# Attention and clustering block, first image: where the score units of the first steps stand between the value products

## The chip, the cores and the metric

The kernel runs on one core of one Trainium2 chip. A core has a matrix engine (TensorE, PE in the profile; its weight loads are the row PEld), a vector engine (VectorE, DVE), a scalar engine for activations (ScalarE, ACT), GpSimd (POOL), and SyncE (SP), which here issues transfers. Each engine runs its own instructions in the order of the program and waits for the others by semaphores. The metric is the device time of one execution in microseconds (us), the median of three runs.

## The reference: what is computed

The input is x of shape (4, 256, 64, 64): four images, 256 channels, N = 4096 positions each. Two layers follow. The change lies in the first, which is self-attention over the positions of one image:

```python
xf = x.reshape(B, Cc, N)
q = jnp.einsum('oc,bcn->bno', wq, xf) + bq            # 32 channels
k = jnp.einsum('oc,bcn->bon', wk, xf) + bk[None, :, None]
attn = jax.nn.softmax(jnp.einsum('bnd,bdm->bnm', q, k), axis=-1)
v = jnp.einsum('oc,bcn->bon', wv, xf) + bv[None, :, None]
out = jnp.einsum('bcn,bmn->bcm', v, attn).reshape(B, Cc, H, W)
return gamma[0] * out + x
```

The second layer, per image, is a group norm, a clustering step (each position is given to one of four centres per head by cosine similarity, centres are averaged and handed back), a second group norm, an MLP 256 to 1024 to 256 with GELU, and two scaled ReLU stages with a 256 to 256 product between them. All is float32.

## The kernel before

The images are worked through one after the other. For each: projections to q, k and v; the attention loop (`weighting`); `cluster`; `mlp`. The projections and the first scores of images 1 to 3 are laid into the clustering and MLP of the image before. Image 0 has no image before it, so `alone` makes its projections and its first scores with nothing beside them.

The attention of an image is cut into 8 query blocks (`nb`) of 512 queries, and for each block into 8 groups (`g`) of 512 keys. A pair of block and group is one unit, `u = 8 * nb + g`, so there are 64 units. The code handles a unit three times, in different places:

- `score(u)` (L359 to L384) makes the 512 x 512 scores. Four 32-row products go side by side into two PSUM tiles of two banks each, `halves[0]` and `halves[1]`. The pool `ps_s` has room for just these two tiles, so the next unit can begin only when both are read. Each half is read twice: ScalarE copies it to an SBUF slot (L377 for the first half, L382 for the second), and VectorE takes the running maximum over keys (L381 from the second half, L384 from the first; for a group 0, L379 alone).
- `exps(u)` (L452 to L468), once the maximum of the block is known: VectorE subtracts it (L460, two halves), ScalarE takes the exponential in place (L463, two halves), GpSimd adds the result to a running total `acc` (L465, L468).
- `weigh(u, av, quarter)` (L470 to L479): the value products. A unit has four quarters of 128 keys. A quarter is two products in the code, which the profile shows as four instructions on TensorE.

`weighting` (L576) runs one step per unit. Step u first issues `exps(u + 1)` and then the four quarters of `weigh(u)`. Between the quarters stand calls `due(u, quarter)` (L569), which issue the score unit, if any, that the table `at` names for this place; after the last score of a block they also call `fold`, the first part of the block's final maximum. Usually it is unit u + 10 (`LEAD`), ahead of quarter 0 of step u. The order of instructions is written out by hand in this way: the scheduler is off (`tc.manual_schedule()`), and each engine gets its instructions in the order in which the Python code runs.

For images 1 to 3 (`b` not zero) the first steps are different: the MLP of the image before has already scored units 0 to 7, and units 8 to 15 are put at the quarter indices 2, 4, 7, 10, 13, 16, 18 and 21, counted from step 0 (`(14 * i + 10) // 5`, L565). For image 0, `alone` scores units 0 to 8. Then L567 puts unit 9 ahead of quarter 0 of step 0 and unit 10 ahead of quarter 2. Image 0 also has a special order in step 0 (L598 to L600): quarters 0 and 1 of the value products are issued ahead of `due(0, 0)`, and the general place (L606 to L609) is skipped. So units 9 and 10 follow each other directly in step 0, after quarter 1. From step 1 on unit u + 10 comes ahead of quarter 0 of step u.

Three other things stand near. After step 1, image 0 runs `early()`, which is `derived` (L194 to L224): some fifteen small VectorE operations on weights of 128 x 2 elements, two square roots on ScalarE that need another function table, two transposes and a small product on TensorE, and two copies of their results. From step 3 on, `biased` steps add the value bias to x on ScalarE (L632), and step 3 fetches the queries of block 2 (L638). And in step 5 `highest` (L433) begins to work out the maximum of block 1, which needs units 8 to 15.

Of the kernel before, what the change touches and what calls it, by code (L numbers as in the profile page):

```python
# [28 lines left out]
RG, GRP = 4, N // NB  # L29
# [16 lines left out]
def attention_then_cluster_block(  # L46
# [78 lines left out]
    def load_mix(b):  # L125
        own_w["mix"] = swap.tile([P, KC, 2, 2 * ED + 32], F32, tag="mix", name=f"mix_{b}")
        for f in range(2):
            nc.sync.dma_start(
                out=own_w["mix"][:, :, f, 16 : 16 + 2 * ED],
                in_=wfv.rearrange("(k p) m -> p k m", p=P),  # L130
            )
# [139 lines left out]
    def attention(b, xs):  # L271
# [76 lines left out]
        def score(u, hooks=None, later=None):  # L348

            nb, g = divmod(u, GRP)  # L350
            q_s, k_s = qs[nb], own["k"]
            pool, tag = (swap, "w1") if u % (SLOTS + 1) == SLOTS else (spool, "s")
            s = slots[u] = pool.tile([P, RG, NB], F32, tag=tag, name=f"s_{b}_{u}")
            halves = [
                ps_s.tile([P, 2, NB], F32, tag="s", name=f"sc_{b}_{u}_{h}") for h in range(2)
            ]
            for r in range(RG):
                rows = slice(r * D, (r + 1) * D)
                nc.tensor.matmul(  # L359
                    halves[r // 2][:, r % 2, :], k_s[rows, g, :], q_s[rows, :], start=True, stop=True  # L360
                )
            if g == 0:
                tops[nb] = work.tile([P, 2, NB], F32, tag="top", bufs=1, name=f"top_{b}_{nb}")
            top = tops[nb]
            if hooks is not None:

                nc.scalar.copy(s[:, 0:2, :], halves[0])
                hooks.append(lambda: nc.scalar.copy(s[:, 2:4, :], halves[1]))
                for h in range(1 if g == 0 else 0, 2):
                    for i in range(2):  # L370
                        later.append(
                            lambda h=h, i=i: nc.vector.tensor_tensor(
                                top[:, i], s[:, i] if g == 0 else top[:, i], s[:, 2 * h + i], ALU.max
                            )
                        )
                return
            nc.scalar.copy(s[:, 0:2, :], halves[0])  # L377
            if g == 0:
                nc.vector.tensor_tensor(top, halves[1], s[:, 0:2, :], ALU.max)  # L379
            else:  # L380
                nc.vector.tensor_tensor(top, halves[1], top, ALU.max)  # L381
            nc.scalar.copy(s[:, 2:4, :], halves[1])  # L382
            if g:
                nc.vector.tensor_tensor(top, halves[0], top, ALU.max)  # L384

        def fold(nb):

            top = tops[nb]
            nc.vector.tensor_tensor(top[:, 0], top[:, 0], top[:, 1], ALU.max)
# [80 lines left out]
        def weigh(u, av, quarter):  # L470
            g = u % GRP
            for c in range(KC):
                nc.tensor.matmul(  # L473
                    av[c],
                    own["v"][:, RG * g + quarter, c * P : (c + 1) * P],
                    slots[u][:, quarter, :],
                    start=(g == 0 and quarter == 0),
                    stop=(g == GRP - 1 and quarter == RG - 1),
                )  # L479

        def gather(nb):

            acc = accs.pop(nb)
            rdens[nb] = work.tile([P, NB], F32, tag="rden", bufs=1, name=f"rden_{b}_{nb}")
            nc.gpsimd.tensor_tensor(rdens[nb], acc[:, 0], acc[:, 1], ALU.add)
# [75 lines left out]
        at = {(u, 0): u + LEAD for u in range(units - LEAD)}  # L561
        if b:
            for i in range(6):
                del at[i, 0]
            at.update({divmod((14 * i + 10) // 5, RG): GRP + i for i in range(8)})  # L565
        else:
            at[0, 2], at[0, 0] = at[0, 0], GRP + 1  # L567

        def due(u, quarter):  # L569
            p = at.get((u, quarter))  # L570
            if p is not None:
                score(p)
                if p % GRP == GRP - 1:
                    fold(p // GRP)

        def weighting(ahead, fill, early):  # L576
            mb, av = None, None

            biased = {u: (i // KC, i % KC) for i, u in enumerate((3, 4, 5, 6, 20, 28, 36, 44))}
            for u in range(units):  # L580
                nb, g = divmod(u, GRP)
                more = nb + 1 < NBLK
                if g == 0:
                    av = [
                        ps_a.tile([P, NB], F32, tag=f"a{c}", name=f"av{c}_{b}_{nb}")
                        for c in range(KC)
                    ]
                if g + 1 < GRP:
                    exps(u + 1)
                else:  # L590
                    gather(nb)
                p = u + LEAD
                if u == units - 4:
                    load_mix(b)
                    load_mlp(b)
                elif u == units - 1:
                    turn_mlp()
                if u == 0 and not b:  # L598
                    weigh(u, av, 0)
                    weigh(u, av, 1)  # L600
                due(u, 0)
                if p - units > 1:
                    ahead()
                if g == GRP - 1 and more:
                    exps(u + 1)
                if u or b:  # L606
                    weigh(u, av, 0)
                    due(u, 1)
                    weigh(u, av, 1)  # L609
                if nb:  # L610
                    if g == 0:
                        total(nb - 1)
                    elif g == 3:
                        add(nb - 1)
                    elif g == 5:
                        seen(nb - 1)
                    elif g == 7:
                        pooled(nb - 1)
                due(u, 2)
                weigh(u, av, 2)  # L620
                if g == GRP - 2 and more:
                    known(nb + 1, mb)
                due(u, 3)
                if g == GRP - 3 and more:
                    mb = highest(nb + 1)
                weigh(u, av, 3)
                if u == 1:
                    early()
                if u in biased:

                    t, c = biased[u]
                    nc.scalar.activation(  # L632
                        xs[t][:, c], xs[t][:, c], AF.Identity, bias=gbv[:, c : c + 1]
                    )
                if u == 2 * GRP + 1:
                    q_four(1)
                if g == 3 and nb + 2 < NBLK:
                    q_block(nb + 2)  # L638
                if g == GRP - 1 and more:
                    clear(nb, av)  # L640

            nb = NBLK - 1
            table(AF.Sqrt)

            den = ps_m.tile([P, NB], F32, tag="m", name=f"den_{b}_{nb}")
            for j in range(4):
                nc.tensor.matmul(
                    den[j * D : (j + 1) * D, :P],
                    ones[:, :D],
                    rdens[nb][:, j * P : (j + 1) * P],  # L650
                    start=True,
                    stop=True,
                )
            fill(2)
            t_s = work.tile([P, KC, NB], F32, tag="t", bufs=1, name=f"t_{b}_{nb}")
            rec = t_s[:, 1, :P]
            nc.vector.reciprocal(rec, den[:, :P])

            inv = ps_m.tile([P, NB], F32, tag="m", name=f"inv_{b}_{nb}")
            for j in range(4):  # L660
                nc.tensor.matmul(
                    inv[:, j * P : (j + 1) * P],
                    ident[:, j * D : j * D + 1].to_broadcast([P, P]),
                    rec,
                    start=True,
                    stop=True,
                )
            rden = rdens[nb]
            nc.scalar.copy(rden, inv)
            fill(6)  # L670
            for c in range(KC):
                yb = block(xs, c, nb)
                nc.vector.tensor_tensor(t_s[:, c], av[c], rden, ALU.mult)
                nc.vector.scalar_tensor_tensor(
                    yb, t_s[:, c], pvc("gamma"), yb, ALU.mult, ALU.add
                )
            seen(nb)
            return stats, cells, lambda: pooled(nb)
# [768 lines left out]
```

## Time and profile before

| what | us |
|---|---|
| median of three runs | 3419.7 (3418.95 to 3419.9) |
| the profiled execution | 3419.29 |
| its span on the core | 3417.5 |
| stretch from 61.5 to 109.5 us, TensorE busy | 44.99 of 48.00 |
| stretch from 109.5 to 285 us, TensorE busy | 175.50 of 175.50 |
| one score unit's maximum over one half (L381), mean | 1.221 |
| one score unit's copy of one half (L377), mean | 1.004 |
| one subtraction of a half (L460), mean | 1.205 |
| one exponential of a half (L463), mean | 1.057 |
| one subtotal on GpSimd (L468), mean | 2.360 |

The page's table of slices shows the same thing at a coarse scale. The span is cut into 40 equal slices, and each digit is the busy share of an engine in tenths:

```profile
PE   8999999999999999999999999999999999999999
DVE  4667764655566766464556676646546766765543
ACT  5555543444555554344455555434446555544444
POOL 2655665210265666521125566652004675672200
PEclk9999999999999999999999999999999999999999
```

A slice is about 85 us. The first one holds the loads, `alone` and the first two steps of image 0's attention loop. A start time and a duration in the timeline are in us from the start of the span; several equal instructions in a row are put together as "x8". A duration of such a group runs to the modelled end of its last instruction, and may overlap the next row by some hundred ns.

### The profile page before, as it was taken

To read this page: it belongs to the slowest core of one execution; us is meant where nothing else is said; L and a number is where in the kernel's file an instruction comes from. 1 tells how busy PE (TensorE), PEld (TensorE's weight loads), DVE (VectorE), ACT (ScalarE), POOL (GpSimd) and SP (SyncE) were. 2 spreads that over 40 slices of the span, in tenths; PEclk is the share of its full clock that TensorE was granted. 3 is DMA by queue.
4 is the path that set the end of the run, shared out by engine and by line. 5 is a ranking of instruction groups with operands and counts; after the bars stand their busy time and mean duration, and the time that the engine had idled before them with its cause. 6 is when DMAs were issued, how large, how long until landed. Compare 5 with 4: busy or idle time off the path is not lost.

```text
span 3417.5 us, 31890 instructions
## 1 busy us (share of the span) xinstructions
PE 3363.0 (98%) x11536; PEld 1663.4 (49%) x11536; DVE 2069.2 (61%) x3219; ACT 1674.2 (49%) x2157; POOL 1490.3 (44%) x807
## 2 busy tenths in 40 slices
PE   8999999999999999999999999999999999999999
PEld 4434445665533444565544344466554343445565
DVE  4667764655566766464556676646546766765543
ACT  5555543444555554344455555434446555544444
POOL 2655665210265666521125566652004675672200
PEclk9999999999999999999999999999999999999999
DMA  2000002000000000100000000010000000010000
GB/s 71 13 13 10 16 7 85 7 19 13 19 13 13 13 13 22 70 7 19 19 16 13 10 13 13 22 70 7 19 19 13 13 13 13 13 36 1 13 19 25
DMA packets 41501, 70.01 MB, mean 20 GB/s; under 512 B 9632, under 2 KB 16896, under 8 KB 41344
## 3 DMA queue, kind: packets, MB, share of 16 engines
q1 hardware_dynamic: 36480, 61.16, 5.3%
q10 hardware_dynamic: 4608, 6.30, 0.8%
q8 instruction: 91, 1.49, 0.2%
q0 software_dynamic: 256, 0.52, 0.1%
q14 instruction: 66, 0.54, 0.1%
HBM read 42.68 MB, written 16.89 MB: 17 GB/s over the span
## 4 chain that ended last, share of the span: by engine, by line
PE 95%; DVE 3%; ACT 1%; issue 0%; DMA 0%; SPq 0%; ACTq 0%; DVEq 0%
PE av L473 53%; PE mo L1204 12%; PE sc L359 8%; PE hu L1197 4%; PE pw L1173 3%; PE hp L1197 3%; PE hq L1197 3%; PE vp L310 2%; PE fv L859 2%; PE op L980 1%; PE qp L329 0%; PE kp L287 0%; DVE vf L868 0%; DVE hs L1233 0%; PE agg L889 0%
## 5 line engine op out<-in xcount | busy, mean ns | idle before, releaser
L473 PE MATMUL av<-s,v 128*128 128x512 f32 x4096 | 1820.5, 598 | 0.6 <-ACT s L463 0.6
L468 POOL TENSOR_TENSOR acc<-acc,s 128x1024 f32<-128x1024 f32 x448 | 1057.3, 2360 | 543.2 <-ACT s L463 524.4
L473 PEld LDWEIGHTS av<-s,v 128*128 128x128 f32 x4096 | 759.8, 190 | 1045.4 <-issue 1035.4
L463 ACT ACTIVATE s<-s 128x1024 f32<-128x1024 f32 x512 | 540.1, 1057 | 592.7 <-DVE s L460 549.7
L460 DVE TENSOR_TENSOR s<-s,mb 128x1024 f32<-128x1024 f32 x512 | 595.5, 1205 | 17.8 <-ACT mb L444 15.9
L1204 PE MATMUL mo<-hs,w 128*128 128x512 f32 x992 | 508.3, 595 | 3.8 <-ACT hs L1226 1.6
L381 DVE TENSOR_TENSOR top<-sc,top 128x1024 f32<-128x1024 f32 x196 | 239.4, 1221 | 377.9 <-PE sc L359 377.8
L1226 ACT ACTIVATE hs<-hs,pv_s 128x256 f32<-128x256 f32 x496 | 251.4, 508 | 361.1 <-DVE hs L1233 350.1
L1233 DVE TENSOR_TENSOR hs<-hu,hs 128x256 f32<-128x256 f32 x372 | 157.7, 424 | 356.2 <-ACT hs L1236 205.5
L377 ACT COPY s<-sc 128x1024 f32<-128x1024 f32 x224 | 224.8, 1004 | 228.8 <-PE sc L359 228.8
L1159 POOL TENSOR_TENSOR xn<-xn 128x256 f32<-128x256 f32 x27 | 23.9, 884 | 682.4 <-DVE xn L1146 488.0
L359 PE MATMUL sc<-q,k 32*128 32x512 f32 x2048 | 294.4, 640 | 3.0 <-ACT s L382 3.0
L384 DVE TENSOR_TENSOR top<-sc,top 128x1024 f32<-128x1024 f32 x196 | 240.0, 1224 | 72.6 <-ACT s L377 59.4
L382 ACT COPY s<-sc 128x1024 f32<-128x1024 f32 x224 | 227.0, 1014 | 66.2 <-DVE top L379 36.1
L465 POOL TENSOR_TENSOR acc<-s 128x1024 f32<-128x1024 f32 x32 | 75.3, 2354 | 366.8 <-ACT s L463 366.7
L1233 DVE TENSOR_TENSOR hs<-hq,hs 128x256 f32<-128x256 f32 x372 | 146.3, 421 | 107.5 <-PE hq L1197 103.2
L1204 PEld LDWEIGHTS mo<-hs,w 128*128 128x128 f32 x992 | 186.9, 190 | 42.6 <-ACT hs L1236 7.8
L359 PEld LDWEIGHTS sc<-q,k 32*128 32x128 f32 x2048 | 81.8, 182 | 193.7 <-issue 141.5
L1197 PE MATMUL hp<-xn,w 128*128 128x256 f32 x496 | 150.6, 385 | 2.6 <-ACT v L318 2.6
L1197 PEld LDWEIGHTS hp<-xn,w 128*128 128x128 f32 x496 | 92.4, 190 | 73.0 <-issue 62.5
L310 PE MATMUL vp<-wv_s,x 128*128 128x256 f32 x512 | 123.4, 387 | 0.2 <-ACT v L318 0.2
L1173 PE MATMUL pw<-xn,wpw_s 128*128 128x512 f32 x248 | 112.0, 594 | 3.4 <-ACT xn L1267 2.2
(219 smaller groups left out, 2737.7 us busy)
## 6 DMA issues: line engine op xcount, KB each, us to landing
x<-in_x SPq DMA_DIRECT2D x32, 512.0 KB, 6.6
out<-xn SPq DMA_DIRECT2D x62, 256.0 KB, 2.1
w<-in_w SPq DMA_DIRECT2D x8, 1024.0 KB, 10.2
mr<-row_mx SPq DMA_DIRECT2D x28, 256.0 KB, 3.1
rden<-row_rd SPq DMA_DIRECT2D x28, 256.0 KB, 3.1
q<-q ACTq DMA_DIRECT2D x96, 64.0 KB, 2.0
mix<-in_wfv SPq DMA_DIRECT2D x8, 192.0 KB, 8.1
q<-q SPq DMA_DIRECT2D x24, 64.0 KB, 2.0
```

What stands on the lines that cost most here:

```text
L359: nc.tensor.matmul(halves[r // 2][:, r % 2, :], k_s[rows, g, :], q_s[rows, :], start=True, stop=True)
L381: nc.vector.tensor_tensor(top, halves[1], top, ALU.max)
L382: nc.scalar.copy(s[:, 2:4, :], halves[1])
L384: nc.vector.tensor_tensor(top, halves[0], top, ALU.max)
L460: nc.vector.tensor_tensor(sh, sh, mxs[nb].unsqueeze(1).to_broadcast([P, 2, NB]), ALU.subtract)
L463: nc.scalar.activation(sh, sh, AF.Exp)
L468: nc.gpsimd.tensor_tensor(acc, acc, s[:, 2 * h : 2 * h + 2], ALU.add)
L473: nc.tensor.matmul(av[c], own["v"][:, RG * g + quarter, c * P : (c + 1) * P], slots[u][:, quarter, :], start=(g == 0 and quarter == 0), st ...
L1197: nc.tensor.matmul(out, w[:, j * P : (j + 1) * P], x, start=True, stop=True)
L1204: yield nc.tensor.matmul(acc[c], w2_s[:, jj, c * P : (c + 1) * P], hs[:, i], start=(j == 0 and i == 0), stop=(j == HID // P // 2 - 1 and i ...
L1226: nc.scalar.activation(dst, src, act, bias=bias)
L1233: nc.vector.tensor_tensor(dst, ps, term, ALU.add)
```

## The change

It concerns image 0 only. The table of score places is set anew for its first steps: the entries for quarter 0 of steps 0 to 5 are taken out, and units 9 to 15 are put at the quarter indices 2, 5, 8, 11, 14, 17 and 20, that is ahead of (step, quarter) (0, 2), (1, 1), (2, 0), (2, 3), (3, 2), (4, 1) and (5, 0). The special order of step 0 is taken out as well, so that step 0 has the general order: due, quarter 0, due, quarter 1, due, quarter 2, due, quarter 3. Nothing is at place (0, 0) any more.

```diff
         else:
-            at[0, 2], at[0, 0] = at[0, 0], GRP + 1
+            for i in range(6):
+                del at[i, 0]
+            at.update({divmod(3 * i + 2, RG): GRP + 1 + i for i in range(7)})
...
-                if u == 0 and not b:
-                    weigh(u, av, 0)
-                    weigh(u, av, 1)
                 due(u, 0)
                 if p - units > 1:
                     ahead()
                 if g == GRP - 1 and more:
                     exps(u + 1)
-                if u or b:
-                    weigh(u, av, 0)
-                    due(u, 1)
-                    weigh(u, av, 1)
+                weigh(u, av, 0)
+                due(u, 1)
+                weigh(u, av, 1)
```

| unit | place before (quarters done) | place after (quarters done) |
|---|---|---|
| 9 | 2 | 2 |
| 10 | 2 | 5 |
| 11 | 4 | 8 |
| 12 | 8 | 11 |
| 13 | 12 | 14 |
| 14 | 16 | 17 |
| 15 | 20 | 20 |
| 16 | 24 | 24 |

## The prediction

> **What bounds the kernel now.** I read the page's first part, then TensorE's waits over the whole span, then the timeline of the stretch that the change reorders, TensorE's rows first and those of the other engines after. Busy time, then TensorE's two longest waits and the one that this change concerns (columns: in total, times, longest):
>
> ```profile
> PE 3363.0 (98%) x11536; PEld 1663.4 (49%) x11536; DVE 2069.2 (61%) x3219; ACT 1674.2 (49%) x2157; POOL 1490.3 (44%) x807
> PE cnt L910 <- DVE scr L829: 9.9, 4, 2.7
> PE kp L287 <- DMA x<-in_x: 9.4, 3, 8.8
> ...
> PE sc L359 <- ACT s L382: 3.0, 1, 3.0
> ```
>
> TensorE is busy for 98% of the span, so a change of order can win only where TensorE stands still. In the weighting loops of all four images scores (L359) wait on their predecessors just once. The stretch table puts it at 61.5 to 109.5 us, where TensorE is busy 44.99 of 48.00 us; from 109.5 to 560 us it is busy in every microsecond. That one wait on TensorE's own row:
>
> ```profile
> 61.52 3.70 PE L473 MATMUL av<-s,v 128*128 128x512 f32 x8 [0.56 <-ACT s L463]
> 65.15 1.65 PE L359 MATMUL sc<-q,k 32*128 32x512 f32 x8
> 69.79 1.53 PE L359 MATMUL sc<-q,k 32*128 32x512 f32 x8 [2.99 <-ACT s L382]
> 71.25 5.29 PE L473 MATMUL av<-s,v 128*128 128x512 f32 x8
> 76.47 1.14 PE L359 MATMUL sc<-q,k 32*128 32x512 f32 x8
> 77.54 7.13 PE L473 MATMUL av<-s,v 128*128 128x512 f32 x16
> ```
>
> Columns are start, duration, then in brackets the idle time and what ended it. These are quarters 0 and 1 of step 0, unit 9, unit 10, quarters 2 and 3, unit 11, and the four quarters of step 1. An undisturbed unit takes 1.07 us from its start to the next one's (76.47 to 77.54), and 16 products take 7.06 us (the chain of waits), so a quarter (4 of them) takes 1.765. Unit 9 could hand over at 65.15 + 1.07 = 66.22; unit 10 starts at 69.79. That is 3.57 us of standstill; the row says 2.99 since it counts from a modelled end.
>
> A second cost follows it, in the weight loads:
>
> ```profile
> 73.97 0.34 PEld L473 LDWEIGHTS av<-s,v 128*128 128x128 f32 x1 [0.52 <-issue]
> 74.66 0.19 PEld L473 LDWEIGHTS av<-s,v 128*128 128x128 f32 x1 [0.35 <-issue]
> ```
>
> Until about 74.4 us a load takes 0.34 us, later 0.19: TensorE runs at half clock after the standstill. From 69.79 to 76.47 pass 6.68 us for work of 1.07 + 2 x 1.765 = 4.60, so 2.08 us are lost. In all 3.57 + 2.08 = 5.65 us is all that the change can take away.
>
> Why unit 10 waits, on VectorE's and ScalarE's rows:
>
> ```profile
> 64.49 2.34 DVE L460 TENSOR_TENSOR s<-s,mb 128x1024 f32<-128x1024 f32 x2
> 66.85 1.23 DVE L381 TENSOR_TENSOR top<-sc,top 128x1024 f32<-128x1024 f32 x1
> 68.85 1.23 DVE L384 TENSOR_TENSOR top<-sc,top 128x1024 f32<-128x1024 f32 x1 [0.78 <-ACT s L377]
> 68.72 1.01 ACT L382 COPY s<-sc 128x1024 f32<-128x1024 f32 x1
> ```
>
> Unit 9's two score tiles are released by L382 (69.73) and L384 (70.08), and unit 10 comes with no product in between. VectorE does step 1's subtraction (L460) ahead of the maxima, and ScalarE its two exponentials ahead of the copies: from the start of L460 to TensorE's release pass 69.79 - 64.49 = 5.30 us. I use that figure again.
>
> [...] 3.57 us of standstill, then about 4.6 us of slow loads. [...] a subtotal on GpSimd ends at 81.50, and a 128x2 VectorE operation started at 80.18 ends at 81.53, although its twin takes 0.16 us:
>
> ```profile
> 76.69 4.81 POOL L468 TENSOR_TENSOR acc<-acc,s 128x1024 f32<-128x1024 f32 x2 [4.97 <-ACT s L463]
> 80.18 1.35 DVE L167 TENSOR_SCALAR dw_d<-pc_s 128x2 f32<-128x2 f32 x1
> 82.46 0.16 DVE L167 TENSOR_SCALAR pw_s<-pc_s 128x2 f32<-128x2 f32 x1
> ```
>
> **The change, part by part.** Nothing is added or dropped: units 9 to 15 only move, 9 and 15 not at all, counted in products. Unit 10 goes from quarter index 2 to 5, 11 from 4 to 8, 12 from 8 to 11, 13 from 12 to 14, 14 from 16 to 17. A unit issues eight TensorE instructions, two ScalarE copies and two VectorE maxima, and no DMA; the key fetch for block 2 (L638, ScalarE's queue) stays at step 3, behind unit 13's copies as before. The q, k and x loads are not passed.
>
> *Unit 9*: same place, same times. TensorE goes on at 66.22 with quarters 2 and 3 and quarter 0 of step 1, whose exponentials (65.73 to 67.92) are in time: 66.22 + 3 x 1.765 = 71.51. *Unit 10* starts there; its tiles are free at 70.08, so 1.43 us of slack. The wait and the half clock go: -5.65 us.
>
> VectorE now does step 2's subtraction (L460) right after unit 9, at 69.99, and ScalarE its exponentials from 71.23. Readers of a unit start 1.23 us after it (76.47 to 77.70), so unit 10's maxima and copies run from 72.74 to about 75.5 behind these. TensorE: 72.58, three quarters, 77.88, then the early weights' transposes (84.68 to 85.09, 0.41), unit 11 at 78.30, three quarters of step 2, and *unit 12* is due at 79.37 + 5.30 = 84.67.
>
> Is unit 11 out by then? In VectorE's queue ahead of its maxima stand the early small operations and step 3's subtraction. The first small one is again held by GpSimd: step 2's subtotals start 1.20 us after their exponential (75.49 to 76.69 before), so at 72.43, and end at 77.24. From the end of that held operation to step 3's subtraction passed 85.64 - 81.53 = 4.11 us before, but 0.73 of it was idle, waiting for the transposes, which are now done at 78.3. So the subtraction starts at 77.27 + 4.11 - 0.73 = 80.65. By the 5.30 us above unit 11 is released at 85.95. Unit 12 waits 85.95 - 84.67 = 1.28 us. That is a new stall: +1.3 us. Bounds: 0 if the early operations slip in between the two subtotals (2.4 us earlier on VectorE); 2.5 if they are held once more for half a subtotal (1.2 us); I take 1.3. [...]
>
> *Units 13 to 15*: unit 12 ends at 87.02; its maxima end near 89.7, step 4's subtraction near 92.0. Unit 13 is due at 87.02 + 3 x 1.765 = 92.3 with 2.6 us of slack; unit 14 after three more at 98.7, its tiles free at about 96.1 although bias (L632) and key fetch stand in between. Unit 15 is due 1.07 + 5.30 later, at 105.1, against 109.43 before. Beyond it the order is untouched, so all later work shifts by the same 4.3 to 4.4 us. Score slots cost nothing: a unit's copies overwrite scores whose products and subtotals are done, and every moved unit comes after more products than before. The maximum for block 1 follows unit 15 as before.
>
> Sum: -5.65 + 1.3 = -4.35 us. The profiled execution took 3419.29 us around a span of 3417.5; its span should become 3413.1. The runs shown have median 3419.7, 0.4 above the profiled one, and the same difference gives 3415.3.
>
> **Rivals.**
> 1. *The full gain.* VectorE gets through the early operations before or between the subtotals, and unit 12 finds its tiles free: 3419.7 - 5.65 = 3414.0. For it: the other images have no early block, and the waits show no such score wait in them. Against it: the 1.35 us row, which shows the hold.
> 2. *Half clock elsewhere.* [...] every later gap (four of 1.7 to 2.7 us at L910, one of 3.2, one of 3.7) falls differently when all shifts by 4.3. One window at half clock costs half of 3.4, 1.7 us; two of them fewer and no new stall give 3414.0 - 3.4 = 3410.6, one more gives 3417.0. Against it: the three runs before differ by 0.95 us[...].
> 3. *The wait only moves, and turns out slower.* Place: unit 12 behind the early operations and step 3's subtraction on VectorE. If that queue is 2.3 us later than I think, the new standstill reaches 3.6 us, the half clock returns with its 2.08, and the gain is used up; that is the deciding point. At a standstill of 5.0 the sum is -5.65 + 5.0 + 2.1 = +1.4: 3421.1. For it: VectorE has the early block, a subtraction and two maxima before unit 12. Against it: every term is a row of this trace.
> 4. *No effect*: with the new wait at 3 to 3.5 us without half clock, 3417 or so. That the edit does not do what it says is out: due positions are explicit, and each of units 9 to 15 is called once.
>
> **How the numbers follow.** Forecast 0.68, rival 1 0.14, rival 2 0.08, rival 3 0.04, rival 4 0.06. Predicted 3415.3 us, which is 0.13% less. A measurement of this kernel can tell about 0.2% (6.8 us) from no change, so the forecast itself, rivals 1 and 4 and most of 3 count as the same: 0.88. Faster by more, below 3412.9, needs rival 2's lucky side or something that I don't see: 0.09. Slower by more: 0.03. The range takes in rivals 1 and 4 and the bounds of the new stall (3414.0 to 3416.6, with 0.5 to either side for runs): 3413.0 to 3418.6.
>
> **What would show it.** Right: no wait of about 3 us at the second unit; weight loads of 0.19 us from 61 us on, without a 0.34 stretch; a wait of some 1.3 us at the fourth unit of the loop, near 86 us, put down to L382 or L384; unit 15 starting near 105 us. Wrong: a wait there of 3 us or more, a stall at unit 10, 11, 13 or 14, or a gain that is not in place by 110 us.

## The result, and the profile after

| | before | after |
|---|---|---|
| median, us (22 runs each) | 3419.57 | 3414.82 |
| lowest to highest, us | 3416.03 to 3421.31 | 3410.07 to 3417.73 |
| profiled execution, us | 3419.29 | 3412.34 |
| its span, us | 3417.5 | 3410.6 |

The ratio of the runs is 0.9984, with a 95% interval of 0.9978 to 0.9991: a gain of 0.16%, inside the 0.2% that was called no change.

The two profiled spans differ by 6.9 us, more than the medians do. To read the change itself I use a **yardstick** in the rest of this text: from the start of unit 8's scores to the start of unit 16's on TensorE. Unit 8 comes ahead of everything that moved, and unit 16 has the same place in both kernels. It is 117.56 - 59.82 = 57.74 us before and 112.45 - 58.70 = 53.75 us after, so the change takes away 3.99 us. Of the other 2.9 us, 1.12 is an earlier start (unit 8 at 58.70 instead of 59.82; over all twelve profiles it starts between 58.27 and 59.82, ahead of anything that was moved), and about 1.7 is an estimate for one stretch of half clock less in the later stages (3.41 us at a granted clock of 0.50, so half of it), whose number differs from profile to profile, as the experiments show.

Busy time in the changed kernel, from the first part of the page:

```profile
PE 3358.4 (98%) x11536; PEld 1661.4 (49%) x11536; DVE 2070.0 (61%) x3219; ACT 1674.5 (49%) x2157; POOL 1490.4 (44%) x807
```

TensorE does the same 11536 products in 4.6 us less busy time, in part because products at half clock count as busy for longer (in the kernel before, eight value products take 5.29 us behind unit 10 and 3.70 ahead of unit 9), behind unit 10 as in the later stages. The waits of TensorE in the changed kernel (total, times, longest), with the wait of scores cut from 3.0 to 0.5 us and the others as they were:

```profile
PE cnt L908 <- DVE scr L827: 9.9, 4, 2.7
PE kp L287 <- DMA x<-in_x: 9.6, 3, 8.7
PE hu L1195 <- DVE hs L1231: 4.7, 5, 3.7
PE gnm_gn L241 <- DVE mv_gn L239: 3.8, 4, 3.2
...
PE sc L359 <- ACT s L382: 0.5, 1, 0.5
```

TensorE's timeline of the stretch in the changed kernel, units 9, 10 and 12, and 15 at the end:

```profile
64.03 1.65 PE L359 MATMUL sc<-q,k 32*128 32x512 f32 x8
65.61 5.42 PE L473 MATMUL av<-s,v 128*128 128x512 f32 x12
70.96 1.14 PE L359 MATMUL sc<-q,k 32*128 32x512 f32 x8
...
78.86 5.42 PE L473 MATMUL av<-s,v 128*128 128x512 f32 x12
84.73 1.47 PE L359 MATMUL sc<-q,k 32*128 32x512 f32 x8 [0.45 <-ACT s L382]
86.14 5.42 PE L473 MATMUL av<-s,v 128*128 128x512 f32 x12
...
104.32 1.14 PE L359 MATMUL sc<-q,k 32*128 32x512 f32 x8
```

Unit 10 now follows three quarters and starts without a wait. Unit 12 waits. Three quarters take 70.96 - 65.61 = 5.35 us, so it was due at 78.86 + 5.35 = 84.21; it starts 0.52 later, and then takes 1.41 us to the next product instead of 1.07. Together the stall costs 0.86 us. The group of its weight loads is longer as well, but the products after it are at full clock (1.00 from 84 to 90 us):

```profile
84.73 0.64 PEld L359 LDWEIGHTS sc<-q,k 32*128 32x128 f32 x8 [1.28 <-ACT s L382]
86.67 0.19 PEld L473 LDWEIGHTS av<-s,v 128*128 128x128 f32 x1 [0.24 <-issue]
```

What unit 12 waits for, on VectorE's timeline of the changed kernel, with ScalarE's copy L382 as the last line:

```profile
73.52 1.22 DVE L384 TENSOR_TENSOR top<-sc,top 128x1024 f32<-128x1024 f32 x1
74.66 1.49 DVE L167 TENSOR_SCALAR dw_d<-pc_s 128x2 f32<-128x2 f32 x1
...
79.43 2.34 DVE L460 TENSOR_TENSOR s<-s,mb 128x1024 f32<-128x1024 f32 x2
81.69 1.21 DVE L381 TENSOR_TENSOR top<-sc,top 128x1024 f32<-128x1024 f32 x1
83.80 1.23 DVE L384 TENSOR_TENSOR top<-sc,top 128x1024 f32<-128x1024 f32 x1 [0.89 <-ACT s L377]
83.66 1.02 ACT L382 COPY s<-sc 128x1024 f32<-128x1024 f32 x1
```

The early weight operations hold VectorE from 74.66 to 79.43, step 3's subtraction follows, and only then are unit 11's tiles read. From the subtraction's start to unit 12's start pass 84.73 - 79.43 = 5.30 us, the same figure as at unit 10 before. The two tiles come free one after the other: unit 12's first products start at 84.73, behind the end of L382 (84.68), those for its other tile at 85.08, behind the end of L384 (85.03). This second wait is the 0.34 us by which the unit takes longer.

### The profile page after: what moved, and what is told of

Read it like the earlier page. It is cut to its first block, busy times and chain, and to the rows that moved or that the text cites. A ratio compares the mean times of both kernels' runs of the same rounds, so it can differ in the third digit from the quotient of the medians.

```text
span 3410.6 us, 31890 instructions
## 1 busy us (share of the span) xinstructions
PE 3358.4 (98%) x11536; PEld 1661.4 (49%) x11536; DVE 2070.0 (61%) x3219; ACT 1674.5 (49%) x2157; POOL 1490.4 (44%) x807
## 3 DMA queue, kind: packets, MB, share of 16 engines
q8 instruction: 91, 1.49, 0.2%
## 4 chain that ended last, share of the span: by engine, by line
PE 95%; DVE 3%; ACT 1%; issue 0%; DMA 0%; SPq 0%; ACTq 0%; DVEq 0%
PE av L473 53%; PE mo L1202 12%; PE sc L359 8%; PE hu L1195 4%; PE pw L1171 3%; PE hp L1195 3%; PE hq L1195 3%; PE vp L310 2%; PE fv L857 2%; PE op L978 1%; PE qp L329 0%; PE kp L287 0%; DVE vf L866 0%; DVE hs L1231 0%; PE agg L887 0%
## 5 line engine op out<-in xcount | busy, mean ns | idle before, releaser
L384 DVE TENSOR_TENSOR top<-sc,top 128x1024 f32<-128x1024 f32 x196 | 240.1, 1225 | 72.3 <-ACT s L377 59.6
L382 ACT COPY s<-sc 128x1024 f32<-128x1024 f32 x224 | 227.1, 1014 | 66.2 <-DVE top L379 36.2
```

## The experiments

The yardstick comes from one profile each and isn't touched by what happens in later stages. Where two kernels have the same order in this stretch (before and before with filled gaps, for example) it agrees within 0.02 us. Totals are given for the kernels that were run several times; the other four were run once. Edits are shown against the changed kernel where nothing else is said, and "..." marks lines left out.

| kernel | yardstick, us | total, us |
|---|---|---|
| before | 57.74 | 3419.57 (22 runs) |
| changed | 53.75 | 3414.82 (22 runs) |
| unit 12 one quarter later | 52.89 | |
| early operations at step 9 | 52.48 | 3415.03 (20 runs) |
| the same, units 9 and 10 paired | 57.63 | 3419.20 (12 runs) |
| the same, one quarter between 9 and 10 | 54.26 | |
| general order alone, old table | 59.08 | |
| changed, one subtotal left out | 53.34 | |
| early at step 9, all units one quarter later | 51.98 | 3413.39 (21 runs) |
| the same, later gaps filled | 51.98 | 3407.96 (5 runs) |
| before, later gaps filled | 57.74 | 3413.18 (19 runs) |
| changed, later gaps filled | 53.73 | 3409.49 (7 runs) |

**Unit 12 one quarter later.**

```diff
-            at.update({divmod(3 * i + 2, RG): GRP + 1 + i for i in range(7)})
+            at.update({divmod(q, RG): GRP + 1 + i for i, q in enumerate((2, 5, 8, 12, 15, 17, 20))})
```

> Yardstick: from the start of unit 8's scores to the start of unit 16's on TensorE (57.74 us before, 53.75 after). My theory: unit 12 still waits after the change (0.9 us in all, with a score unit of 1.41 instead of 1.07) because unit 11 is read only behind the early operations and step 3's subtraction; one quarter more (1.7 us) ahead of it covers that. Expected 52.8 us and no wait of a score unit other than unit 9's half a microsecond. Rival: VectorE and ScalarE have no room at this spacing, so the wait moves on to unit 13 or 14 and the yardstick stays at 53.7.

Measured: 111.82 - 58.93 = 52.89 us, and no wait of a score on TensorE's list. The timeline of this kernel has four quarters, then unit 12 at once:

```profile
79.09 7.13 PE L473 MATMUL av<-s,v 128*128 128x512 f32 x16
86.15 1.14 PE L359 MATMUL sc<-q,k 32*128 32x512 f32 x8
87.22 5.42 PE L473 MATMUL av<-s,v 128*128 128x512 f32 x12
```

The wait did not move on: 53.75 - 52.89 = 0.86 us, which is the whole stall of unit 12.

**Early operations at step 9.** The scaling of the value bias, which step 3 needs, goes to step 0; the rest of `early()` runs after step 9.

```diff
-        nc.vector.tensor_scalar(gbv, gbv, pvc("gamma"), None, ALU.mult)
...
+                if u == 0 and not b:
+                    nc.vector.tensor_scalar(gbv, gbv, pvc("gamma"), None, ALU.mult)
...
-                if u == 1:
+                if u == GRP + 1:
                     early()
```

> Yardstick unit 8 to unit 16. My theory: the early weight operations are what makes unit 12 late. Moved to step 9 (the value bias' scaling, needed from step 3, goes to step 0), they take 0.41 us of transposes out of the stretch and the 0.9 us of unit 12's wait with them: 52.4 us, and no new wait at step 9 or 10, where a unit comes only every 8.13 us. Rival: the spacing of three quarters is itself too close; then unit 12 waits as before and only 0.4 goes (53.3). Total time: 3414 within the scatter of half-clock windows (about 1.7 us each).

Measured: 111.95 - 59.47 = 52.48 us. Both parts are there: 0.41 us of transposes and 0.86 us of wait, and no score waits at step 9 or 10. Three quarters are enough for VectorE and ScalarE; only the early block made unit 12 late. The total, 3415.03 us (ratio to before 0.9987, 0.9980 to 0.9994), does not show these 1.3 us.

**Units 9 and 10 paired again**, all else as in the kernel just told.

```diff
+            del at[1, 1]
...
                 score(p)
+                if p == GRP + 1 and not b:
+                    score(p + 1)
```

> As the kernel with the early operations at step 9, but unit 10 directly behind unit 9 again; the other units stay evenly spaced. My theory: the pair alone makes the cost that the change removed: a standstill of 3.6 us and, after it, half clock with 2.0 us of loss. Yardstick 52.4 + 4.8 = 57.2 us. Rival 1, the whole uneven table is needed for it: 53 to 54. Rival 2, the standstill costs only itself and half clock has another cause: 55.3.

Measured: 116.09 - 58.46 = 57.63 us, 5.15 more than without the pair, and 3419.20 us in all (ratio to before 1.0002, 0.9993 to 1.0010). The pair brings the old time back with everything else new. TensorE's timeline and weight loads in this kernel:

```profile
63.79 1.65 PE L358 MATMUL sc<-q,k 32*128 32x512 f32 x8
68.73 1.70 PE L358 MATMUL sc<-q,k 32*128 32x512 f32 x8 [3.29 <-ACT s L381]
70.35 11.99 PE L472 MATMUL av<-s,v 128*128 128x512 f32 x24
```

```profile
72.22 0.34 PEld L472 LDWEIGHTS av<-s,v 128*128 128x128 f32 x1 [0.52 <-issue]
73.08 0.29 PEld L472 LDWEIGHTS av<-s,v 128*128 128x128 f32 x1 [0.52 <-issue]
73.60 0.19 PEld L472 LDWEIGHTS av<-s,v 128*128 128x128 f32 x1 [0.24 <-issue]
```

The standstill and the stretch of slow loads of the kernel before are back, two parts of one cost.

**One quarter between 9 and 10.** The table is (2, 3, 8, 11, 14, 17, 20), with the early operations at step 9.

> As the kernel with the early operations at step 9, but unit 10 only one quarter behind unit 9 instead of three. My theory: the release of unit 9's tiles stays where it is, so the standstill shrinks from 3.6 to some 1.2 us and is too short for half clock; yardstick 52.4 + 1.5 = 53.9 us, weight loads at 0.19 us throughout. Rival: any standstill of this kind brings half clock with its 2 us: 55.9 us, with loads of 0.34 us after it.

Measured: 113.01 - 58.75 = 54.26 us. The timeline shows unit 10 and, in the weight loads, full speed behind it:

```profile
69.02 1.47 PE L358 MATMUL sc<-q,k 32*128 32x512 f32 x8 [1.38 <-ACT s L381]
70.42 8.85 PE L472 MATMUL av<-s,v 128*128 128x512 f32 x20
```

```profile
69.02 0.65 PEld L358 LDWEIGHTS sc<-q,k 32*128 32x128 f32 x8 [2.21 <-ACT s L381]
70.96 0.19 PEld L472 LDWEIGHTS av<-s,v 128*128 128x128 f32 x1 [0.24 <-issue]
71.39 0.19 PEld L472 LDWEIGHTS av<-s,v 128*128 128x128 f32 x1 [0.24 <-issue]
```

A standstill of 1.4 us costs 54.26 - 52.48 = 1.78 us: itself and 0.34 us of a stretched unit, without half clock. As at unit 12 of the changed kernel, these 0.34 us are the wait for the second tile, whose last reader (the maximum) ends at 69.31, 0.34 us after the copy that releases the first.

In the kernel before, TensorE stands still for 3.57 us, and half clock follows from 71.07 on; here it stands still for 1.4 us (67.6 to 69.0), and the loads of the value products behind unit 10 take 0.19 us. That its place in time played no part was not shown. So in this one profile the two further quarters between 9 and 10 are needed for the wait, not for the clock.

**The general order in step 0 alone**, with the table of before.

```diff
-            for i in range(6):
-                del at[i, 0]
-            at.update({divmod(3 * i + 2, RG): GRP + 1 + i for i in range(7)})
+            at[0, 2], at[0, 0] = at[0, 0], GRP + 1
```

> The second part of the change alone: the general order in step 0, with the table of before (unit 9 ahead of quarter 0, unit 10 ahead of quarter 2, then every four). Yardstick, start of unit 8 to start of unit 16 on TensorE. My theory: unit 9 now stands directly behind unit 8, and the standstill moves there (unit 8's second tile comes free some 4.8 us after unit 8 ends), with half clock after it; about 58.3 us, no better than the 57.74 before, so the two parts belong together. Rival: the two quarters between 9 and 10 are enough by themselves, 54 to 55.

Measured: 117.61 - 58.53 = 59.08 us, 1.3 more than before. Unit 9 stands directly behind unit 8 and waits twice, once for each of its halves, and the products after it take 5.43 us to unit 10 where 3.63 are usual (the granted clock is half for 6.83 us from 63.22 on):

```profile
62.07 1.13 PE L359 MATMUL sc<-q,k 32*128 32x512 f32 x4 [2.41 <-ACT s L377]
64.38 2.08 PE L359 MATMUL sc<-q,k 32*128 32x512 f32 x4 [1.18 <-ACT s L382]
66.39 5.50 PE L473 MATMUL av<-s,v 128*128 128x512 f32 x8
```

So the special order of step 0 had a use with the old table. With the new table it makes no difference: nothing stands at the places (0, 0) and (0, 1), so by the code either order issues the same instructions in the same sequence. What changes the kernel is the table alone.

**One subtotal left out.** GpSimd's additions of unit 2 to the running totals of image 0 are left out, so one group is missing from the denominators of one block.

```diff
-            else:
+            elif u != 2 or b:
                 for h in range(2):
                     nc.gpsimd.tensor_tensor(acc, acc, s[:, 2 * h : 2 * h + 2], ALU.add)
```

> The changed kernel with GpSimd's additions of unit 2 to the running total left out in every block's unit 2 of the first image's first block (step index 2 only), so the denominators lack one group there; nothing else differs. My theory: VectorE's first early operation is held by GpSimd's subtotal (1.49 us in the changed kernel); without it, it takes 0.16 us, step 3's subtraction starts 1.3 us earlier relative to unit 8, and unit 12 no longer waits: yardstick 52.8 us. Rival: the operation is long for another reason (its operand, or the first use of the weights); then it stays at 1.3 to 1.5 us and the yardstick at 53.7.

Measured: the first small operation falls from 1.49 to 0.16 us, as my theory had it, but the yardstick only to 112.41 - 59.07 = 53.34 us. VectorE's timeline, and then ScalarE's:

```profile
75.03 0.16 DVE L167 TENSOR_SCALAR dw_d<-pc_s 128x2 f32<-128x2 f32 x1
76.38 0.17 DVE L170 RECIPROCAL dw_d<-dw_d 128x2 f32<-128x2 f32 x1 [1.19 <-ACT dw_d L168]
...
79.39 2.34 DVE L460 TENSOR_TENSOR s<-s,mb 128x1024 f32<-128x1024 f32 x2
```

```profile
74.85 1.28 ACT L168 ACT_TABLE_LOAD   x1
76.14 0.20 ACT L168 ACTIVATE dw_d<-dw_d 128x2 f32<-128x2 f32 x1
```

Counted from unit 8, VectorE gets through its operation 1.3 us sooner and then waits 1.19 us for the square root, which waits for ScalarE's table load. From unit 8 to step 3's subtraction pass 20.32 us instead of 20.73. The hold by GpSimd is real, but it lies beside a table load of nearly the same length, and alone it is worth 0.41 us.

**Early at step 9, and all units one quarter later**: the table is (3, 6, 9, 12, 15, 18, 21).

> Early operations at step 9, and units 9 to 15 at 3, 6, 9, 12, 15, 18, 21, one quarter later each, so that unit 9 too finds its tiles free. Yardstick unit 8 to unit 16: 52.48 - 0.5 (unit 9's half wait) = 51.95 us with no wait of a score unit. Rival: the wait only moves to the end of the stretch, where unit 16 follows unit 15 after three quarters; 52.5. Total: 1.8 us below the changed kernel if the half-clock windows of the later stages (1.7 us each) fall alike, so 3413, which the scatter of these windows can hide.

Measured: 110.86 - 58.88 = 51.98 us; no score waits any more. The total is 3413.39 us (ratio to before 0.9980, 0.9974 to 0.9987), with 21 runs between 3408.52 and 3416.09.

**The scatter.** That spread lies between runs of one and the same kernel, so the order of units can't explain it. The trace records the granted clock; half clock (0.50) comes there, apart from the end of the kernel, in stretches of 3.41 us or twice that (in the kernel before 3.41 from 630.86, 6.83 from 2521.84). Behind the stretch of the yardstick, and again apart from the end, the profiled executions have six windows of 3.41 us at half clock, a double one counted as two (before), five (changed), eight (unit 12 later), eight (early at step 9), six (paired), six (one quarter), six (order alone), three (subtotal) and eight (the last one). If each costs half its length, 1.71 us, which is an estimate, then total less start of unit 8, less yardstick, less windows leaves 3290.7 to 3292.3 us in all nine, where the totals themselves go from 3409.4 to 3419.3. For before: 3419.29 - 59.82 - 57.74 - 6 x 1.71 = 3291.5. To test this, products of constants, whose results are overwritten, were put into gaps behind which such windows appear. The edit is against the kernel just told:

```diff
+    def warm(ps, n):
+        for _ in range(n):
+            nc.tensor.matmul(
+                ps, ident, wpw_s.rearrange("p k m -> p (k m)"), start=True, stop=True
+            )
...
         cnt_p = ps_a.tile([P, NB], F32, tag="a1", name=f"cnt_{b}")
+        warm(cnt_p, 3 if b < B - 1 else 1)
...
+        if which == "gn2" and b == B - 1:
+            warm(ps1, 3)
```

> As the previous one, with products of constants (0.86 us each, results overwritten) in TensorE's later gaps: three ahead of the count in the clustering of images 0 to 2, one in that of image 3, three ahead of the second group norm of image 3. My theory: what scatters the total by up to 7 us is the number of half-clock windows behind these gaps, 5 to 8 of 1.7 us each in the profiles so far; with the gaps filled only the one behind the 3.7 us wait of the MLP of image 2 remains, so 1 to 2 windows, a total of 3405 to 3409 and a narrower scatter. Rival: the scatter comes from elsewhere (transfers); then the median stays near 3413 to 3415 or rises by the added products, and the scatter stays.

Measured: 3407.96 us (ratio to before 0.9965, 0.9953 to 0.9978), five runs from 3407.50 to 3408.13, and one window left besides the end (a mean clock of 0.96 from 2500 to 2540 us, 1.00 in 560 to 700, 1420 to 1560, 2270 to 2400 and 3100 to 3405). The clustering of image 0 on TensorE's timeline, first without the filling (all units one quarter later), then with it:

```profile
624.03 2.82 PE L909 MATMUL cnt<-scr,ones 128*96 128x64 f32 x16 [2.71 <-DVE scr L828]
626.78 2.79 PE L888 MATMUL agg<-vf,sim 128*32 128x96 f32 x64
```

```profile
621.29 2.74 PE L236 MATMUL cnt<-wpw_s,ident 128*128 128x512 f32 x6
624.16 1.57 PE L918 MATMUL cnt<-scr,ones 128*96 128x64 f32 x16
625.66 1.53 PE L896 MATMUL agg<-vf,sim 128*32 128x96 f32 x64
```

The filled gap ends 0.13 us later, 0.09 of which was there at unit 8, and the same 80 small products take 3.0 us instead of 5.5. This version is faster than both kernels, by 0.34% against the kernel before.

With 1.71 us for each window the saving would be overstated, though. Seven windows fewer than in the profile of the same kernel without filling should give 12 us, and the profiled execution is 8.57 us shorter (3416.07 to 3407.50). Around the last gap, where TensorE has other waits too, the double window that all nine profiles have was worth only 1.3 us: the product behind that gap comes 7.29 us earlier than without filling, the MLP's products after the window 8.59 us earlier.

**The gaps filled in before and in the changed kernel**, with nothing else different.

> The kernel before, with products of constants in the later gaps as in the previous run with them. My theory: this takes the scatter of the later half-clock windows out of both kernels, so that the change alone can be read from totals. Previous such kernel 3408.0 with a yardstick of 51.98 us; here 57.74, so 3413.7. Rival: filling the gaps works only at that kernel's timing; then the scatter is as before and the median near 3418.

> The changed kernel with the same products in the later gaps. My theory: 3408.0 + 53.75 - 51.98 = 3409.7 us, 4.0 us below the kernel before with these products, with a scatter of under 1 us: the change's own worth without half-clock chance in the later stages. Rival: part of the measured 4.8 us between the two medians comes from the later stages; not seen here, then the difference is 4.0; if the difference is 5 or more, the yardstick misses something.

Measured: 3413.18 us (3411.85 to 3415.63) and 3409.49 us (3408.79 to 3410.47), with yardsticks of 57.74 and 53.73. The ratios to the kernel before are 0.9983 (0.9976 to 0.9990) and 0.9972 (0.9961 to 0.9984). The two totals differ by 3.69 us, near the 4.0 of the yardstick. With less scatter in both this is a better measure of the change's worth than the 4.75 us between the medians above. The scatter shrank less than I expected: 3.8 us over 19 runs, and 1.7 us over 7 where I had said under 1; the profiles still have one and two windows in the later stages (mean clocks of 0.96 and 0.91 from 2500 to 2540 us). The half clock behind unit 10 in the first of the two, one window long in this profile (a mean clock of 0.97 from 61.5 to 120 us), may add to its scatter; I did not test that apart.

## Why the prediction was right, and which terms were off

*The mechanism* was right. The pair of units costs a standstill and then half clock, and three quarters between them remove both: shown by the paired kernel, which gives 57.63 us and the old total.

*Half clock.* It does not follow every stall of a score: shown, in one profile, by the kernel with one quarter between (1.4 us, loads of 0.19 us behind it), where the kernel before has 3.57 us and loads of 0.34. The 2.08 us put on it are 1.97 when eight instructions are taken at their usual 3.64 us, and 0.34 of these are again the wait for a second tile (70.13 instead of 69.79, behind the end of L384 at 70.08). So half clock itself cost 1.63 us. The prediction read 4.6 us of slow loads, counted from the start of unit 10; the recorded clock is half only from 71.07 to 74.48, one window of 3.41 us, and half of that is 1.71.

*What can be removed.* The prediction let unit 9 hand over at 66.22, 1.07 us after its start, and so counted 3.57 us of standstill. In the changed kernel unit 9 takes 65.61 - 64.03 = 1.58 us in the same place, since its second half, which starts at 64.55, waits for unit 8's last copy. ScalarE's timeline of the changed kernel, and the same wait in the weight loads of the kernel before:

```profile
63.49 1.01 ACT L382 COPY s<-sc 128x1024 f32<-128x1024 f32 x1 [1.29 <-DVE top L379]
```

```profile
65.67 0.30 PEld L359 LDWEIGHTS sc<-q,k 32*128 32x128 f32 x4 [0.22 <-ACT s L382]
```

0.51 us stayed. The kernel with all units one quarter later removes it. This is the largest wrong term, and the 1.65 us of unit 9 in the kernel before, against 1.14 of unit 11, already showed it.

*Unit 12's stall.* Place and cause were as said: the early block ahead of step 3's subtraction, shown by the kernel with that block at step 9. Its size was put at 1.28 us; it is 0.86, of which 0.52 is the wait ahead of it and 0.34 the wait for its second tile, which the prediction did not have. The release was right within 0.1 us (85.95 predicted; 84.73 measured, which is 85.85 when unit 8 starts as before). But unit 12 itself came 0.7 us later than predicted, by unit 9's half wait and 0.05 us more for each group of three quarters, and so waited less. That a stall of this size brings no half clock was an estimate of mine; here none followed.

*The hold by GpSimd.* The prediction made this the thing that sets the start of the early operations. The kernel without that subtotal shows the hold (0.16 us for the first small operation instead of 1.49), but also that it is only half of the answer: ScalarE's table load, 1.28 us, stands beside it. By what means GpSimd holds VectorE was not shown. Rival 1 (VectorE slipping through early) would have given about 0.4 us, not 1.3.

*The slack of units 10, 13, 14 and 15* was as predicted: none waited.

*The sum.* 4.35 us predicted, 3.99 on the yardstick: 3.57 of standstill and 1.97 of half clock, less the 0.51 that stayed at unit 9, the 0.86 at unit 12, and some 0.2 that the prediction did not count. The stretch now has eight groups of value products instead of seven, and each group costs about 0.2 us beyond its products: 8, 12 and 16 instructions take 3.64, 5.35 and 7.06 us. That the sum came so near is in part luck: unit 9 cost 0.5 us more than said and unit 12 0.4 us less. The median's drop of 4.75 us, and the 0.5 us by which it came under the predicted 3415.3, lie within the scatter of half-clock windows. Rival 2 was right that these windows change the profiled executions by several us (three to eight of them, an estimated 1.71 us each); that they fall differently because all later work shifts was not shown. What was wrong in it was the argument that three runs within 0.95 us show them to be harmless; 22 runs of the same kernel spread over 5.3 us.

## What to carry to other kernels

Two users of the same pair of score tiles need as much other work between them as the tiles' readers take, and the readers' queue counts: here a subtraction and two exponentials stood ahead of the copies and maxima, and from the subtraction's start to the release passed 5.30 us. When work is spread out evenly, look for the one-off block in the readers' queue, and leave one place more there. Here a standstill of 3.6 us on TensorE cost its length and two more us behind it, 1.6 of them by half clock. Where a gap can't be closed, try filling it with products that nobody needs, as was done in three kernels here (one of them went from 3413.39 to 3407.96 us), and measure small changes only after that.

## What the runs showed of the hardware

I had not expected these gaps to matter so much outside the stretch that was changed. Within a profile the half-clock stretches begin whole multiples of 3.413 us apart (in the kernel before at 71.07, 630.86, 1477.37 and so on). In the profiles of the two kernels this grid lies differently against the program: from the start of image 0's count products to half clock pass 630.86 - 629.87 = 0.99 us before and 626.63 - 624.78 = 1.85 us after. The changed kernel scattered by 7.7 us (0.22%) over 22 runs.

In the kernel before, a wait of 2.71 us ahead of the count products was followed by half clock in images 0 and 1 (from 630.86 and from 1477.37) and by full clock in image 2, whose 16 products begin at 2321.55 and take 1.57 us. In the changed kernel image 1 is the one without (a wait of 2.70 us, products at 1470.44). Even the 1.74 us wait ahead of the last image's count had half clock behind it in one profile and not in another: the same 16 products take 2.07 us with it (all units one quarter later) and 1.57 without (before):

```profile
3138.31 2.07 PE L909 MATMUL cnt<-scr,ones 128*96 128x64 f32 x16 [1.74 <-DVE scr L828]
3142.59 1.57 PE L910 MATMUL cnt<-scr,ones 128*96 128x64 f32 x16 [1.74 <-DVE scr L829]
```

The wait of 1.4 us between the long value products was not followed by half clock in the one profile that has it. The work around these gaps differs, so the runs give no single length at which half clock begins. Filling four count gaps and one of 3.2 us left 0.6 us of scatter in five runs. Whether a shorter filling would do was not tried.
